# One of a block's seven products becomes seven quarter-size products, with partial sums copied inside PSUM

## The chip, the core and the metric

The kernel runs on one core of a Trainium2 chip. Its time is the device time of one execution in microseconds (us); the median of several runs counts. A core has TensorE (PE, matrix products into PSUM), VectorE (DVE), ScalarE (ACT), GpSimd (POOL) and SyncE (SP, which here issues most DMA transfers). Each engine works through its own queue in order; semaphores make one wait for another.

## The reference

The input x is 32 images of 14x14 points with 512 channels, all float32. Only the first half of the computation matters for the change; it ends in a residual sum, a group norm and a grouped 3x3 convolution.

```python
for i in range(18):                                   # on the group-normed x
    nx = gelu(einsum('bhwc,cd->bhwd', x, block_w[i]) + block_b[i])   # 512 x 512
    if i in (11, 14, 17):                             # targets
        pooled = nx.mean(axis=(1, 2))
        h = gelu(pooled @ fc1_w[t] + fc1_b[t])
        gates = softmax((h @ fc2_w[t] + fc2_b[t]).reshape(-1, 3, 512), axis=1)
        nx = nx + gammas[t] * einsum('bac,bahwc->bhwc', gates, anchors)
    x = nx
    if i in (1, 4, 9):                                # anchors
        anchors.append(x)
```

## The kernel before

**Tiling.** Channels lie on the partitions, in four chunks of 128. A tile is two images, N = 392 points; a pair is two tiles, and there are 8 pairs. A "quarter" is an SBUF tile of 128 partitions x 2 chunks x 392 points: `q[h][n]` is half h of the channels of tile n. A pair's activations are thus a 2x2 array of quarters, and a 512x512 weight is a 2x2 array of 256x256 corners `a11, a12, a21, a22`. `qpool` holds 38 quarters, `ps_b` 6 banks of PSUM.

**A block** is one layer i for one pair p: a 2x2 by 2x2 product, done in seven products instead of eight (Strassen's scheme in Winograd's form). `sums(k, j)` makes the four weight sums `s[0..3]` on VectorE for pair 0 and stores them; later pairs load them from `skeep`. `pre_adds` makes the four activation sums `t[0..3]` of the next block on VectorE, each from two quarters or from a quarter and an earlier sum. `block(k)` then issues the seven products; each is 4 matmuls of 128x128 by 128x392 (2 output chunks d x 2 input chunks kk), and each float32 matmul shows in the trace as two instructions. The sums of products are kept in PSUM banks X, Y, Z or copied to SBUF by ScalarE (`save`, line 473) and added there by VectorE (`add`, line 477); `gelu` (lines 453 and 460) writes the new quarters. In a target block `gelu` works by image, so that it can sum up the pooled values.

**Order.** `steps` lists all 144 blocks, pairs interleaved, and one step without a block (GAP). A block has 7 ticks, and after each product `run(tick)` issues whatever a calendar holds for that tick: loading and norming of the next pair, the gates of the target blocks (`gate_hidden`, `gate_logits`, `gate_softmax`, `gate_base`, `gate_part`, `gate_last`, `gate_add`), statistics and stores of a finished pair, building of the convolution's weights, and the convolution's units (`unit_load`, `unit_taps` with tile `cps`, `unit_sum`, `unit_out`). `put` finds the first tick with room for a task:

```python
ROOM = {"dve": (1.7, 0.0, 3.4, 3.4, 1.7, 0.0, 0.0), "act": (1.0, 0.8, 1.5, 1.5, 1.0, 0.8, 0.8)}
```

These are microseconds of VectorE and ScalarE for each of the 7 ticks. Inside a tick the order in which the program issues is the order in each queue.

**Head and drain.** The first pair is loaded, turned by TensorE (tile `tpi`), its statistics are taken, and the scale is a power on POOL followed by one Newton step on VectorE; 20 small matmuls (`warm`) are issued before the first block. After the last block `drain()` orders the remaining gates, norm and convolution units with a list scheduler. For chunks named in `BYPE` the output is turned by TensorE (`turn_out`, tile `tpo`) and stored in whole rows by `store_rows`; for the others VectorE transposes it (`unit_out`) and eight or so smaller stores follow.

Of the kernel before, what the change touches and what calls it, by code (L numbers as in the profile page):

```python
# [8 lines left out]

F32 = mybir.dt.float32  # L10
AF = mybir.ActivationFunctionType
ALU = mybir.AluOpType
# [7 lines left out]
def kernel(  # L20
# [20 lines left out]
    nc = tc.nc  # L41
    P = 128
    B, H, W, C = x.shape
    HW = H * W
# [27 lines left out]
    qpool = ctx.enter_context(tc.tile_pool(name="qpool", bufs=38))  # L72
    tmp = ctx.enter_context(tc.tile_pool(name="tmp", bufs=6))
    inpool = ctx.enter_context(tc.tile_pool(name="inpool", bufs=3))
# [40 lines left out]

    ROOM = {"dve": (1.7, 0.0, 3.4, 3.4, 1.7, 0.0, 0.0), "act": (1.0, 0.8, 1.5, 1.5, 1.0, 0.8, 0.8)}
    TAIL = {"dve": 3.0, "act": 3.6}
# [114 lines left out]

    def scales_newton(d, lo=0, hi=NR):
        ve, y, e, mr = d["ve"][:, lo:hi], d["y"][:, lo:hi], d["e"][:, lo:hi], d["mr"]
        nc.vector.tensor_mul(e, y, y)
        nc.vector.tensor_mul(e, e, ve)
        nc.vector.tensor_scalar(e, e, -0.5, 1.5, ALU.mult, ALU.add)
        nc.vector.tensor_mul(mr[:, 1, lo:hi], y, e)
        nc.vector.scalar_tensor_tensor(
            mr[:, 2, lo:hi], mr[:, 0, lo:hi], -1.0, mr[:, 1, lo:hi], ALU.mult, ALU.mult  # L240
        )
# [104 lines left out]
    def plan_start(p):  # L346

        t0 = NP7 * at_step[p, 0]
        parts = [(2 * p + n, c) for n in range(2) for c in range(NCK)]
        NIN = 3  # L350
        a = t0 - LEAD
        at(a - 30, copy_in, p)
        turned = []
        b = 0
        for j, (t, c) in enumerate(parts):
            at(t0 - LEAD - 6 if j < NIN else turned[j - NIN], load_blocks, t, c)
            turned.append(put(max(a, turned[j - NIN] + 4 if j >= NIN else 0), {"dve": 0.45 + c % NH * 0.15}, turn_blocks, t, c))
            a = turned[j]
        for j, (t, c) in enumerate(parts):
            b = max(b, put(turned[j // NH * NH + NH - 1], {"dve": 0.7}, stats_in, t, c))  # L360
        b = put(b + 1, {"dve": 0.8}, lambda: whole(scales_mean(pst[p])))
        b = put(b + 1, {"dve": 0.2}, lambda: whole(scales_rstd(pst[p])))
        b = put(b + 2, {"dve": 0.8}, lambda: scales_newton(pst[p]))
        e = b
        for c in range(NCK):
            e = max(e, put(b, {"dve": 1.6}, norm_in, p, c))
        b = e

        assert b < t0
        at(t0 - 1, take_start, p)  # L370

# [33 lines left out]

    def pre_adds(p, name):

        q = cur[p]
        t = ts[p] = []
        for j in range(4):  # L410
            t.append(quarter(f"t{j}_{name}"))
            i0, i1 = [
                lambda: (q[0][1], q[0][0]),
                lambda: (q[1][1], t[0]),
                lambda: (q[1][1], q[0][1]),
                lambda: (q[1][0], t[1]),
            ][j]()
            nc.vector.tensor_tensor(t[j], i0, i1, ALU.subtract)  # L418

    def block(k):  # L420
        p, i = steps[k]
        if i == GAP:
            for tick in range(NP7 * k, NP7 * (k + 1)):
                run(tick)
            pre_adds(steps[k + 1][0], f"{k + 1}")
            return
        name = f"{p}_{i}"
        tick = NP7 * k
        w = wts.pop(k)
        s, q, t = w["s"], cur[p], ts[p]  # L430
        dst = [[None, None], [None, None]]
# [4 lines left out]

        def product(acc, lhsT, rhs, first):
            for d in range(NH):
                for kk in range(NH):
                    nc.tensor.matmul(  # L440
                        acc[d][:, :N], lhsT=lhsT[:, kk, d * P : (d + 1) * P],
                        rhs=rhs[:, kk, :], start=first and kk == 0, stop=kk == NH - 1,
                        skip_group_check=not first,
                    )

# [24 lines left out]

        def save(cs, acc):
            for d in range(NH):
                nc.scalar.copy(cs[d], acc[d][:, :N])  # L473

        def add(cs, acc):
            for d in range(NH):
                nc.vector.tensor_tensor(cs[d], acc[d][:, :N], cs[d], ALU.add)  # L477

        X = bank("x")
        product(X, w["a11"], q[0][0], True)  # L480
        c1 = temps(1)
        save(c1, X)
        run(tick)
        Y = bank("y")
        product(Y, w["a12"], q[1][0], True)
        add(c1, Y)
        gelu(0, 0, c1)
        run(tick + 1)
        product(X, s[1], t[1], False)
        c2 = temps(2)  # L490
        save(c2, X)
        run(tick + 2)
        Z = bank("z")
        product(Z, s[0], t[0], True)
        c3 = temps(3)
        save(c3, Z)
        run(tick + 3)
        product(X, s[2], t[2], False)
        add(c3, X)
        gelu(1, 1, c3)  # L500
        run(tick + 4)
        product(Z, s[3], q[1][1], False)
        add(c2, Z)
        gelu(0, 1, c2)
        run(tick + 5)
        product(X, w["a22"], t[3], False)
        gelu(1, 0, [X[d][:, :N] for d in range(NH)])
        cur[p] = dst
        run(tick + 6)
        if k + 1 < len(steps) and steps[k + 1][1] != GAP:  # L510
            pre_adds(steps[k + 1][0], f"{k + 1}")
        if i in ANCHORS:
# [161 lines left out]
    def plan_head(p, i):  # L674
# [19 lines left out]
        a = t1 + 2  # L694
        while room("dve", a) < 2.2:
            a += 1
        at(a, gate_logits, k, name, box)
        return put(a, {"dve": 2.2}, lambda: whole(gate_softmax(ti, name, box)))

# [223 lines left out]
    def unit_taps(m, u):  # L923
# [3 lines left out]
        for g in range(2):  # L927
            xv = d["xs"][:, g, 1].rearrange("p (b h) -> p b h", h=H)
            pv = ps[:, g * 2 * NV : (g + 1) * 2 * NV].rearrange("p (b h) -> p b h", h=H)
            for j, dy in enumerate((1, 0, 2)):  # L930
                lo, hi = max(0, 1 - dy), min(H, H + 1 - dy)
                nc.tensor.matmul(  # L932
                    pv[:, :, lo:hi], lhsT=bw[:, g, dy],
                    rhs=xv[:, :, lo + dy - 1 : hi + dy - 1],
                    start=j == 0, stop=j == 2, skip_group_check=True,
                )
# [51 lines left out]

    def store_rows(m, c):
        nc.scalar.dma_start(  # L990
            out[m * BI : (m + 1) * BI, :, :, c * P : (c + 1) * P].rearrange("b h w d -> (b h) w d"),
            outs.pop((m, c)),
        )
# [15 lines left out]
    done = []  # L1009

    def plan_unit(m, u, tk, ahead, stay=False):
        b = tk - ahead
# [5 lines left out]
        a = max(b + 2, tk)  # L1018
        while room("dve", a + 1) < 0.65:
            a += 1  # L1020
        at(a, unit_taps, m, u)
        b = put(a + 1, {"dve": 0.65}, unit_sum, m, u)
        b = put(b, {"dve": 0.6}, unit_out, m, u)
        done.append((a, b))
# [34 lines left out]
    def drain():  # L1059
# [47 lines left out]
        for c in range(NCK):  # L1107
# [40 lines left out]
            else:  # L1148
                for p, d in ((PK, dk), (PL, dl)):
# [11 lines left out]
                  nbytes=0.8e6)  # L1161
        xs, outp, ofirst, BYPE = [], [], None, (2, 3, 4)
        for mm, u in [(m - 1, u) for u in range(NGAP, NU)] + [(m, u) for u in range(NU)]:
# [29 lines left out]
            if ul == UC - 1 and (mm - (NBAT - 2)) * NCK + c not in BYPE:  # L1193
# [8 lines left out]
                if ofirst:  # L1202
                    ofirst.free = t
            elif ul == UC - 1:
                ofirst.free = Task(
                    "ACT", 0.6, lambda mm=mm, c=c: store_rows(mm, c), [o], nbytes=0.8e6
                )
# [56 lines left out]


    for s in range(TS):
        for n in range(2):
            load_in(n, s, qpool, "q", nc.sync if n == 0 else nc.scalar)
    load_block(0)
    brow = load_biases()  # L1270
    for b in range(NI):
# [3 lines left out]
        for n in range(2):  # L1275
            for c in range(NCK):
                stats_in(n, c, (b,))
    whole(scales_mean(pst[0]))
    whole(scales_rstd(pst[0]))
    for j in range(4):  # L1280
        sums(0, j)
    turn_biases(brow)

    warm = aux("warm")
    for j in range(20):
        nc.tensor.matmul(warm[:, :P], lhsT=ident, rhs=gmask, start=True, stop=True)  # L1286
    scales_newton(pst[0])
    for c in range(NCK):
        norm_in(0, c, (0,), nc.vector)
        norm_in(0, c, (1,), nc.scalar)  # L1290
    take_start(0)
    pre_adds(0, "0")


    NGAP = 6
    LEAD = 42
    for k in range(len(steps)):
# [5 lines left out]
        if k > 0:  # L1303
            at(NP7 * (k - 1), load_block, k)
            for tk, j in ((4, 0), (4, 1), (4, 2), (5, 3)) if p == 0 else ((2, 1), (3, 0), (4, 2), (5, 3)):
                at(NP7 * (k - 1) + tk, sums, k, j)
            if p == 0:
                left["dve"][NP7 * (k - 1) + 4] = 0.0
        if i in TARGETS:
            at(NP7 * (k - 1 if k == len(steps) - 1 else k) + 4, load_gates, k)  # L1310
            for tk, us in enumerate((0.8, 0.0, 1.5, 1.5, 0.5, 0.0, 0.0)):
                left["act"][NP7 * k + tk] = us
# [4 lines left out]
    for p in range(NPAIR):  # L1317
        plan_differences(p)
        for i in TARGETS[:-1]:
            a = plan_gates(p, i, plan_head(p, i), [[0, 1], [2, 3]])  # L1320
            assert a < NP7 * at_step[p, i + 1], (p, i, a, NP7 * at_step[p, i + 1])
    for p in range(NPAIR):
# [53 lines left out]
```

## Time and profile before

| | us |
|---|---|
| median of 3 runs | 2941.75 (2938.26 to 2943.97) |
| the profiled execution's own time | 2944.35 |
| its span | 2942.6 |
| TensorE busy in the span | 2905.9 |
| VectorE busy | 1827.2 |
| ScalarE busy | 1425.1 |
| first product starts at | 22.57 |
| last product ends at | about 2836.7 |

The page of a profile gives busy times of the engines, the chain of work that ended last, and groups of like instructions with their source line. The list of waits says which engine's instruction waited for what: microseconds in all, times, longest. The timeline lists instructions in order, runs of like ones merged: start, duration, engine, line, operation, output<-inputs, shape, count, and in brackets the idle time before it with what ended it. Matmuls overlap, so that the distance between two starts says more than the duration. PEld is TensorE's loading of weights; it runs beside PE.

### The profile page before, as it was taken

Reading aid. Unit: us, or ns where it says so; the run is one execution under the profiler, and the core shown is the slowest. Engines: PE = TensorE matmul, PEld = TensorE weight load, DVE = VectorE, ACT = ScalarE, POOL = GpSimd, SP = SyncE. Lnnn points to the kernel's source line nnn. Section 1 sums busy time; section 2 is a strip of 40 time slices with the busy share of each in tenths; the row PEclk is TensorE's granted clock in tenths of the full one; section 3 lists DMA queues with packets and bytes.
Section 4 is the critical chain, followed back from the end, with each engine's and each line's share of the span. In section 5 each row is a group of like instructions: output and inputs, shape, how many; then the busy total and the mean of one; then the engine's idle time right before and its main releaser. Section 6 shows DMA issues by size and latency. Waiting matters only on the chain.

```text
span 2942.6 us, 31539 instructions
## 1 busy us (share of the span) xinstructions
PE 2905.9 (99%) x9693; PEld 1775.3 (60%) x9693; DVE 1827.2 (62%) x3512; ACT 1425.1 (48%) x3281; POOL 78.4 (3%) x60
## 2 busy tenths in 40 slices
PE   9999999999999999999999999999999999999997
PEld 5555555555555665666666666666665655556666
DVE  6887777755377454774547745576455763545676
ACT  4445455555455454454544544445455454544551
POOL 0000000000000000000000000000000000000000
PEclk9999999999999999999999999999999999999999
DMA  5544455644565455654657546566465753443676
GB/s 183 164 148 152 163 171 151 189 124 127 154 168 180 128 173 163 184 162 131 185 151 187 169 138 183 142 190 169 130 189 149 182 150 115 126 148 107 189 211 159
DMA packets 471817, 469.44 MB, mean 160 GB/s; under 512 B 237555, under 2 KB 300130, under 8 KB 471650
## 3 DMA queue, kind: packets, MB, share of 16 engines
q1 hardware_dynamic: 458482, 449.77, 51.5%
q0 software_dynamic: 4608, 12.85, 2.5%
q10 hardware_dynamic: 8560, 4.82, 0.6%
q8 instruction: 78, 1.28, 0.2%
q14 instruction: 89, 0.73, 0.1%
HBM read 388.29 MB, written 90.28 MB: 163 GB/s over the span
## 4 chain that ended last, share of the span: by engine, by line
PE 97%; DMA 2%; DVE 1%; issue 0%; ACT 0%; SPq 0%; DVEq 0%
PE x L440 51%; PE z L440 26%; PE y L440 13%; PE cps L932 4%; PE lps L571 1%; DMA x<-x2d 1%; PE hps L554 1%; DMA w<-in_L_conv_fc_w_dram 0%; PE warm L1286 0%; PE tpi L309 0%; DVE x L921 0%; PE mps_b L208 0%; PE tpo L972 0%; PE mps_a L208 0%; PE vps_a L208 0%
## 5 line engine op out<-in xcount | busy, mean ns | idle before, releaser
L440 PE MATMUL x<-t,s 128*128 128x392 f32 x2304 | 809.8, 494 | 0.0
L453 ACT ACTIVATE o<-c,bias 128x392 f32<-128x392 f32 x720 | 437.3, 620 | 656.1 <-DVE c L477 648.5
L440 PEld LDWEIGHTS x<-t,s 128*128 128x128 f32 x2304 | 433.5, 190 | 302.2 <-issue 0.5
L477 DVE TENSOR_TENSOR c<-x,c 128x392 f32<-128x392 f32 x288 | 160.4, 565 | 486.2 <-PE x L440 411.3
L473 ACT COPY c<-x 128x392 f32<-128x392 f32 x576 | 278.2, 484 | 352.1 <-PE x L440 347.4
L440 PE MATMUL x<-t,w 128*128 128x392 f32 x1152 | 403.2, 493 | 0.0
L440 PE MATMUL z<-t,s 128*128 128x392 f32 x1152 | 402.9, 492 | 0.0
L440 PE MATMUL z<-o,s 128*128 128x392 f32 x1088 | 380.9, 493 | 0.0
L440 PE MATMUL y<-o,w 128*128 128x392 f32 x1088 | 380.4, 492 | 0.0
L440 PE MATMUL x<-o,w 128*128 128x392 f32 x1088 | 380.3, 492 | 0.0
L440 PEld LDWEIGHTS z<-t,s 128*128 128x128 f32 x1152 | 218.6, 190 | 158.8 <-DMA s<-skeep 0.7
L440 PEld LDWEIGHTS x<-t,w 128*128 128x128 f32 x1152 | 218.4, 190 | 158.6
L477 DVE TENSOR_TENSOR c<-y,c 128x392 f32<-128x392 f32 x288 | 162.1, 565 | 237.1 <-PE y L440 147.5
L418 DVE TENSOR_TENSOR t<-o,o 128x784 f32<-128x784 f32 x272 | 264.1, 971 | 65.8 <-ACT o L453 63.9
L440 PEld LDWEIGHTS y<-o,w 128*128 128x128 f32 x1088 | 206.6, 190 | 151.1
L440 PEld LDWEIGHTS x<-o,w 128*128 128x128 f32 x1088 | 206.6, 190 | 148.9
L440 PEld LDWEIGHTS z<-o,s 128*128 128x128 f32 x1088 | 206.2, 190 | 149.5
L418 DVE TENSOR_TENSOR t<-o,t 128x784 f32<-128x784 f32 x272 | 264.4, 972 | 4.7
L473 ACT COPY c<-z 128x392 f32<-128x392 f32 x288 | 139.6, 485 | 203.9 <-PE z L440 203.8
L477 DVE TENSOR_TENSOR c<-z,c 128x392 f32<-128x392 f32 x288 | 156.4, 560 | 95.0 <-PE z L440 94.7
L460 ACT ACTIVATE o<-c,bias 128x196 f32<-128x196 f32 x288 | 129.5, 450 | 92.9 <-DVE c L477 92.4
L453 ACT ACTIVATE o<-x,bias 128x392 f32<-128x392 f32 x240 | 136.7, 581 | 68.2 <-PE x L440 62.8
(119 smaller groups left out, 2027.0 us busy)
## 6 DMA issues: line engine op xcount, KB each, us to landing
w<-in_L_conv_block_w_dram SPq DMA_DIRECT2D x144, 1024.0 KB
s<-skeep SPq DMA_DIRECT2D x504, 256.0 KB
x2d<-xc SPq DMA_DIRECT2D x116, 224.0 KB
x<-x2d SPq DMA_DIRECT2D x104, 224.0 KB
skeep<-s SPq DMA_DIRECT2D x72, 256.0 KB
xkeep<-xt SPq DMA_DIRECT2D x32, 392.0 KB
o<-xkeep POOLq DMA_DIRECT2D x32, 392.0 KB, 6.0
bw<-band SPq DMA_DIRECT2D x32, 384.0 KB
```

What stands on the lines that cost most here:

```text
L418: nc.vector.tensor_tensor(t[j], i0, i1, ALU.subtract)
L440: nc.tensor.matmul(acc[d][:, :N], lhsT=lhsT[:, kk, d * P : (d + 1) * P], rhs=rhs[:, kk, :], start=first and kk == 0, stop=kk == NH - 1, sk ...
L453: nc.scalar.activation(o[:, d, :], srcs[d], AF.Gelu_apprx_tanh, bias=bias[:, r : r + 1])
L460: nc.scalar.activation(o[:, d, sl], srcs[d][:, sl], AF.Gelu_apprx_tanh, bias=bias[:, r : r + 1], accum_out=pooled[:, c, m : m + 1],)
L473: nc.scalar.copy(cs[d], acc[d][:, :N])
L477: nc.vector.tensor_tensor(cs[d], acc[d][:, :N], cs[d], ALU.add)
L554: nc.tensor.matmul(hps[:, :NB4], lhsT=w1[:, kk, :], rhs=box["pooled"][:, kk, :], start=(kk == 0), stop=(kk == NCK - 1),)
L571: nc.tensor.matmul(lps[:, m * NB4 : (m + 1) * NB4], lhsT=w2[:, m * P : (m + 1) * P], rhs=h, start=True, stop=True,)
L932: nc.tensor.matmul(pv[:, :, lo:hi], lhsT=bw[:, g, dy], rhs=xv[:, :, lo + dy - 1 : hi + dy - 1], start=j == 0, stop=j == 2, skip_group_chec ...
```

## The change

Product s0 x t0 is itself a 2x2 by 2x2 product: `s[0]` is cut into four 128x128 corners `a`, `t[0]` into four corners `b` of 128x196 (a half h of the points, chunk kk). It is done by the same scheme in seven inner products of 128x128 by 128x196. For that four weight sums `u` (`inner_sums`, kept in `ukeep` for later pairs) and four activation sums `v` (in `pre_adds`) are needed. Partial sums stay in PSUM: ScalarE copies X to Y and one corner of Z to another, and TensorE adds the next products onto the copies. The second product is added onto Y, so that `gelu(0, 0)` reads PSUM and the temporaries c1 and their VectorE adds are gone. One partial sum, f, goes to SBUF and is added to both corners of Z's second bank by VectorE.

With it: t0 and v of the next block are made before the seventh product instead of after it; `tmp` has 4 buffers for 6; the calendar's `ROOM` and due times are other; convolution units go only into ticks 1 to 4 of a block, and their bank is cleared once; the first pair's scale comes from an integer guess and three Newton steps on VectorE; six warm-up matmuls of 392 columns replace 20 of 128; the last chunk's output is turned by TensorE and stored in two halves.

```diff
-    tmp = ctx.enter_context(tc.tile_pool(name="tmp", bufs=6))
+    tmp = ctx.enter_context(tc.tile_pool(name="tmp", bufs=4))
...
-    ROOM = {"dve": (1.7, 0.0, 3.4, 3.4, 1.7, 0.0, 0.0), "act": (1.0, 0.8, 1.5, 1.5, 1.0, 0.8, 0.8)}
+    ROOM = {"dve": (3.3, 1.9, 1.4, 1.8, 1.4, 0.6, 0.0), "act": (1.5, 0.75, 0.75, 0.8, 1.5, 1.5, 1.5)}
...
+    def scales_guess(d):
+        ps = group_sums(f"vps_{d['name']}", d["dv"], NR)
+        yield
+        nc.vector.tensor_scalar(d["ve"], ps, 1.0 / HW, 1e-5, ALU.mult, ALU.add)
+        nc.vector.tensor_scalar(
+            d["y"].bitcast(I32), d["ve"].bitcast(I32), -0.5, float(0x5F3759DF), ALU.mult, ALU.add
+        )
+    def scales_newton(d, lo=0, hi=NR, times=1):
         ve, y, e, mr = d["ve"][:, lo:hi], d["y"][:, lo:hi], d["e"][:, lo:hi], d["mr"]
-        nc.vector.tensor_mul(e, y, y)
-        nc.vector.tensor_mul(e, e, ve)
-        nc.vector.tensor_scalar(e, e, -0.5, 1.5, ALU.mult, ALU.add)
-        nc.vector.tensor_mul(mr[:, 1, lo:hi], y, e)
+        for i in range(times):
+            nc.vector.tensor_mul(e, y, y)
+            nc.vector.scalar_tensor_tensor(e, e, -0.5, ve, ALU.mult, ALU.mult)
+            o = y if i < times - 1 else mr[:, 1, lo:hi]
+            nc.vector.scalar_tensor_tensor(o, e, 1.5, y, ALU.add, ALU.mult)
...
-        assert b < t0
-        at(t0 - 1, take_start, p)
+        assert b < t0 - 1
+        at(t0 - 2, take_start, p)
...
+    ukeep = [tc.dram_tile([P, 4 * P], F32, name=f"ukeep{i}") for i in range(NB)]
+    def inner_sums(k):
+        p, i = steps[k]
+        d = wts[k]
+        u = d["u"] = spool.tile([P, 4, P], F32, tag="u", name=f"u_{k}")
+        if p > 0:
+            nc.sync.dma_start(u.rearrange("p j d -> p (j d)"), ukeep[i])
+            return
+        a = corners(d["s"][0], P)
+        for j, (i0, i1) in enumerate((
+            (a[1][0], a[0][0]), (a[1][1], u[:, 0]), (a[1][1], a[1][0]), (a[0][1], u[:, 1]),
+        )):
+            nc.vector.tensor_tensor(u[:, j], i0, i1, ALU.subtract)
+        nc.sync.dma_start(ukeep[i], u.rearrange("p j d -> p (j d)"))
+    def corners(t, n):
+        return [[t[:, kk, h * n : (h + 1) * n] for kk in range(NH)] for h in range(2)]
+    def pre_adds(p, q, name, js):
+        t = ts.setdefault(p, {})
+        for j in js:
+            t[j] = quarter(f"t{j}_{name}")
             i0, i1 = [
                 lambda: (q[0][1], q[0][0]),
                 lambda: (q[1][1], t[0]),
...
                 lambda: (q[1][0], t[1]),
             ][j]()
             nc.vector.tensor_tensor(t[j], i0, i1, ALU.subtract)
+            if j == 0:
+                v = t["v"] = quarter(f"v_{name}").rearrange("p k (n x) -> p (k n) x", x=HW)
+                b = corners(t[0], HW)
+                for l, (i0, i1, op) in enumerate((
+                    (b[1][0], b[1][1], ALU.add), (v[:, 0], b[0][0], ALU.subtract),
+                    (b[0][0], b[1][0], ALU.subtract), (b[0][1], v[:, 1], ALU.subtract),
+                )):
+                    nc.vector.tensor_tensor(v[:, l], i0, i1, op)
...
+        def part(acc, d, lhsT, rhs, first=False):
+            for kk in range(NH):
+                nc.tensor.matmul(
+                    acc[d][:, :N], lhsT=lhsT[:, kk, d * P : (d + 1) * P],
+                    rhs=rhs[:, kk, :], start=first and kk == 0, stop=kk == NH - 1,
+                    skip_group_check=True,
+                )
+        def product(acc, lhsT, rhs):
             for d in range(NH):
-                for kk in range(NH):
-                    nc.tensor.matmul(
-                        acc[d][:, :N], lhsT=lhsT[:, kk, d * P : (d + 1) * P],
-                        rhs=rhs[:, kk, :], start=first and kk == 0, stop=kk == NH - 1,
-                        skip_group_check=not first,
-                    )
+                part(acc, d, lhsT, rhs)
...
-        def save(cs, acc):
-            for d in range(NH):
-                nc.scalar.copy(cs[d], acc[d][:, :N])
+        def save(cs, acc, ds=range(NH)):
+            for d in ds:
+                nc.scalar.copy(cs[d][:, :N], acc[d][:, :N])
         def add(cs, acc):
             for d in range(NH):
                 nc.vector.tensor_tensor(cs[d], acc[d][:, :N], cs[d], ALU.add)
+        a, b, u, v = corners(s[0], P), corners(t[0], HW), w["u"], t["v"]
+        Z = []
+        def corner(d, n):
+            return Z[d][:, n * HW : (n + 1) * HW]
+        def inner(d, n, lhsT, rhs, first=False):
+            nc.tensor.matmul(
+                corner(d, n), lhsT=lhsT, rhs=rhs, start=first, stop=True, skip_group_check=True
+            )
         X = bank("x")
-        product(X, w["a11"], q[0][0], True)
-        c1 = temps(1)
-        save(c1, X)
+        Y = bank("y")
+        for d in range(NH):
+            part(X, d, w["a11"], q[0][0], True)
+            save(Y, X, (d,))
+        Z += bank("z")
+        inner(1, 0, u[:, 0], v[:, 0], True)
+        inner(1, 1, a[0][0], b[0][0])
+        f = tmp.tile([P, N], F32, tag="c", name=f"f_{name}")[:, :HW]
+        nc.scalar.copy(f, corner(1, 0))
+        nc.scalar.copy(corner(0, 0), corner(1, 1))
         run(tick)
-        Y = bank("y")
-        product(Y, w["a12"], q[1][0], True)
-        add(c1, Y)
-        gelu(0, 0, c1)
+        part(Y, 0, w["a12"], q[1][0])
+        inner(0, 0, a[0][1], b[0][1])
+        inner(1, 1, u[:, 1], v[:, 1])
+        nc.scalar.copy(corner(1, 0), corner(1, 1))
+        part(Y, 1, w["a12"], q[1][0])
+        gelu(0, 0, [Y[d][:, :N] for d in range(NH)])
         run(tick + 1)
-        product(X, s[1], t[1], False)
         c2 = temps(2)
-        save(c2, X)
+        part(X, 0, s[1], t[1])
+        save(c2, X, (0,))
+        inner(1, 0, a[1][1], v[:, 3])
+        inner(1, 1, u[:, 2], v[:, 2])
+        nc.scalar.copy(corner(0, 1), corner(1, 1))
         run(tick + 2)
-        Z = bank("z")
-        product(Z, s[0], t[0], True)
+        part(X, 1, s[1], t[1])
+        save(c2, X, (1,))
+        inner(0, 1, u[:, 3], b[1][1])
+        both = Z[1][:, :N].rearrange("p (n x) -> p n x", n=2)
+        nc.vector.tensor_tensor(
+            both, both, f.unsqueeze(1).to_broadcast([P, 2, HW]), ALU.add
+        )
         c3 = temps(3)
         save(c3, Z)
         run(tick + 3)
-        product(X, s[2], t[2], False)
+        product(X, s[2], t[2])
         add(c3, X)
         gelu(1, 1, c3)
         run(tick + 4)
-        product(Z, s[3], q[1][1], False)
+        product(Z, s[3], q[1][1])
         add(c2, Z)
         gelu(0, 1, c2)
         run(tick + 5)
-        product(X, w["a22"], t[3], False)
+        pn = steps[k + 1][0] if k + 1 < len(steps) and steps[k + 1][1] != GAP else None
+        if pn is not None:
+            qn = dst if pn == p else cur[pn]
+            pre_adds(pn, qn, f"{k + 1}", (0,))
+        product(X, w["a22"], t[3])
         gelu(1, 0, [X[d][:, :N] for d in range(NH)])
         cur[p] = dst
         run(tick + 6)
-        if k + 1 < len(steps) and steps[k + 1][1] != GAP:
-            pre_adds(steps[k + 1][0], f"{k + 1}")
+        if pn is not None:
+            pre_adds(pn, qn, f"{k + 1}", (1, 2, 3))
...
-                    start=j == 0, stop=j == 2, skip_group_check=True,
+                    start=g == 0 and j == 0, stop=j == 2, skip_group_check=True,
...
+    def fits(tick):
+        return steps[tick // NP7][1] == GAP or 1 <= tick % NP7 <= 4
...
+        while not fits(a) or room("dve", a + 1) < 0.65:
...
-        xs, outp, ofirst, BYPE = [], [], None, (2, 3, 4)
+        xs, outp, ofirst, BYPE = [], [], None, (2, 3, 4, 7)
...
+            elif u == NU - 3 and mm == m:
+                Task("ACT", 0.6, lambda mm=mm, c=c: store_rows(mm, c, 0, P // 2), [o], nbytes=0.4e6)
...
+    def keep_busy(n):
+        for j in range(n):
+            banks.append(ps_b.tile([P, 512], F32, tag="b", name="warm"))
+            nc.tensor.matmul(
+                banks[-1][:, :N].rearrange("p (j x) -> p j x", j=NCK), lhsT=ident,
+                rhs=ident[:, : N // NCK].unsqueeze(1).to_broadcast([P, NCK, N // NCK]),
+                start=True, stop=True,
+            )
+    keep_busy(3)
...
-    whole(scales_mean(pst[0]))
-    whole(scales_rstd(pst[0]))
-    for j in range(4):
+    for j, parts in enumerate((scales_mean(pst[0]), scales_guess(pst[0]))):
+        next(parts)
         sums(0, j)
+        whole(parts)
+    scales_newton(pst[0], times=3)
     turn_biases(brow)
-
-    warm = aux("warm")
-    for j in range(20):
-        nc.tensor.matmul(warm[:, :P], lhsT=ident, rhs=gmask, start=True, stop=True)
-    scales_newton(pst[0])
-    for c in range(NCK):
-        norm_in(0, c, (0,), nc.vector)
-        norm_in(0, c, (1,), nc.scalar)
+    keep_busy(3)
+    for n in range(2):
+        for c in range(NCK):
+            norm_in(0, c, (n,), nc.vector if (c + n) % 2 == 0 else nc.scalar)
     take_start(0)
-    pre_adds(0, "0")
+    pre_adds(0, cur[0], "0", range(4))
+    inner_sums(0)
+    for j in range(2, 4):
+        sums(0, j)
...
-    LEAD = 42
+    LEAD = 47
...
-            for tk, j in ((4, 0), (4, 1), (4, 2), (5, 3)) if p == 0 else ((2, 1), (3, 0), (4, 2), (5, 3)):
+            for tk, j in ((3, 0), (3, 1), (4, 2), (5, 3)):
                 at(NP7 * (k - 1) + tk, sums, k, j)
+            at(NP7 * (k - 1) + 4, inner_sums, k)
             if p == 0:
-                left["dve"][NP7 * (k - 1) + 4] = 0.0
+                for tk, us in ((3, 0.5), (4, 0.0), (5, 0.0)):
+                    left["dve"][NP7 * (k - 1) + tk] = us
...
-            for tk, us in enumerate((0.8, 0.0, 1.5, 1.5, 0.5, 0.0, 0.0)):
+            for tk, us in enumerate((1.2, 0.0, 0.3, 0.8, 0.3, 0.2, 0.0)):
```

## The prediction

> **What bounds the kernel now.** I read the page first, then TensorE's waits, then stretches of the timeline. The page:
>
> ```profile
> span 2942.6 us, 31539 instructions
> ...
> PE 2905.9 (99%) x9693; PEld 1775.3 (60%) x9693; DVE 1827.2 (62%) x3512; ACT 1425.1 (48%) x3281; POOL 78.4 (3%) x60
> ...
> PE 97%; DMA 2%; DVE 1%; issue 0%; ACT 0%; SPq 0%; DVEq 0%
> ```
>
> TensorE is busy for 99% and the chain that ended last is 97% TensorE; VectorE and ScalarE have 38% and 52% to spare. A busy TensorE could still hide stalls, so its waits:
>
> ```profile
> PE cps L932 <- DMA x<-x2d: 10.8, 4, 6.2
> PE tpi L309 <- DMA xin<-in_x_dram: 4.2, 1, 4.2
> PE cps L932 <- DVE x L921: 3.0, 4, 1.2
> ```
>
> The list has no product of a block (L440): the largest waits lie in the head (tpi) and the drain (cps), before 22.6 us and after 2836 us. In the 144 blocks the time is TensorE's own streaming. What a pass costs is read from the distance between starts, since the durations overlap:
>
> ```profile
> 998.74 2.33 PE L932 MATMUL cps<-x,bw 128*128 128x224 f32 x12
> 1000.91 2.80 PE L440 MATMUL x<-t,s 128*128 128x392 f32 x8
> ...
> 1008.81 2.80 PE L440 MATMUL x<-o,w 128*128 128x392 f32 x8
> ...
> 1010.38 0.49 ACT L473 COPY c<-x 128x392 f32<-128x392 f32 x1 [0.78 <-PE x L440]
> ...
> 1011.44 2.80 PE L440 MATMUL y<-o,w 128*128 128x392 f32 x8
> ...
> 1298.42 1.84 PE L571 MATMUL lps<-h,w 128*128 128x4 f32 x16
> ...
> 1300.13 2.88 PE L440 MATMUL x<-t,s 128*128 128x392 f32 x8
> ```
>
> A product is 8 instructions (4 float32 matmuls, two passes each): 1011.44-1008.81 = 2.63 us, 329 ns a pass of 392 columns. A conv unit is 12 passes, 4 of 224 and 8 of 208 columns, mean 213.3: 2.17 us, 181 ns. The lps passes, 4 columns, follow each other in 1.71/16 = 107 ns: that is the floor that a weight load sets. So above the floor a pass costs its columns: (329-181)/(392-213.3) = 0.83 ns a column, about 4 ns fixed.
>
> **The change, part by part.**
>
> *Streaming.* Gone in each block: product s0 x t0, 8 passes of 392 columns, 2.63 us. New: 7 matmuls of 196 columns, 14 passes. By the line above 196 columns cost 181-17.3x0.83 = 166 ns, over the 107 floor; 14x166 = 2.33 us. Saved 0.30 to 0.31 us (rounding of the starts), over 144 blocks 43 to 45; I take 44 us.
>
> Here a rule speaks against the change. The Trainium skill, "TensorE: Matmul & The Clock Gate", section "What overlaps and what doesn't", has a weight load overlap running matmuls only if they use other row groups; all of these use the full array. Then every pass pays load and stream, with the page's load of 128/1.2 = 107 ns: 14x(107+163) = 3.78 against 8x(107+327) = 3.47 us, a loss of 0.31 us a block, 45 us in all. The rows decide: a load is listed for every pass, yet 392 columns take 329 ns, not 434, and the conv passes 181, not 285, though six more short passes a block are just where it would hurt. I use the rows.
>
> *New waits on ScalarE.* Before, no product waited closely for ScalarE. Now a12 x q10 is added onto ScalarE's copy Y, and an inner product onto a copied quarter of Z. Count from the block's start T: a11 ends T+2.63; two inner products T+3.29; Y's first half T+4.61; two more inner T+5.27; Y's second half T+6.59. A copy starts 0.26 us after its last pass has left the issue (1010.38, against 1008.81+4x0.329 = 1010.13). A copy of 392 columns takes 0.48; one of 196 has as nearest row L314's 0.34, 0.31 in sequence. PSUM as the target has no row; I bound it by 0.2 and 0.6 and take 0.31. So Y's halves are there at T+2.1 and T+3.4, f at T+3.9, the corner copy at T+4.2. The first is wanted at T+3.29, the corner at T+4.61: slack 0.4 us, the thinnest in every block. The later corner copies wait behind `gelu` and calendar work and still have over 0.7 us. So nothing stalls in an ordinary block. Behind these waits TensorE's own queue stands, and with it everything.
>
> *Gate blocks.* ScalarE's room in ticks 4, 5 and 6 goes from 1.0, 0.8 and 0.8 to 1.5: two `gate_last` in each instead of one. The block after a target, before:
>
> ```profile
> 1302.74 0.25 DVE L607 SCALAR_TENSOR_TENSOR g<-ex,gam,ssum 128x32 f32<-128x32 f32 x1
> ...
> 1303.70 1.03 DVE L477 TENSOR_TENSOR c<-x,c 128x392 f32<-128x392 f32 x2
> ...
> 1304.30 1.13 ACT L453 ACTIVATE o<-c,bias 128x392 f32<-128x392 f32 x2 [2.18 <-DVE c L477]
> ...
> 1305.34 0.79 ACT L656 ACTIVATE gq<-o,g 128x196 f32<-128x196 f32 x2
> ...
> 1307.28 0.79 ACT L656 ACTIVATE gq<-o,g 128x196 f32<-128x196 f32 x2
> ...
> 1307.98 1.04 ACT L453 ACTIVATE o<-x,bias 128x392 f32<-128x392 f32 x2
> ...
> 1308.92 0.80 ACT L656 ACTIVATE gq<-o,g 128x196 f32<-128x196 f32 x2
> ...
> 1309.68 0.49 ACT L473 COPY c<-x 128x392 f32<-128x392 f32 x1
> ```
>
> ScalarE runs nearly gap-free from the first gelu on, and its copy at 1309.68 comes just when its half product is ready (1308.11, the block's start, +1.32+0.26). With a double `gate_last` (1.50 us in the trace) three times: add at 1303.0 (no gate_part before it now), gelu 1303.6-1304.75, gates to 1306.2, gelu to 1307.35, gates to 1308.8, gelu to 1309.8, gates to 1311.25, save Y to 1311.75. The next block starts at 1308.11, so Y's half is wanted at 1311.4: a stall of 0.4 us with the handing over. There are 23 such blocks (16 for targets 11 and 14, 7 for 17): +9 us; ends 0 (gates an instruction earlier) and 25 (softmax or an add 0.6 us later).
>
> *VectorE.* Gone: two adds onto c1 (0.565 each). New: four v of 196 columns, one add over both corners (0.56, like L477), for pair 0 also four u of 128. From L418 (784: 971 ns) and L664 (392: 561) a 196-column add is 0.36, some 0.28 back to back. Net +0.6 us a block of 18.1, for pair 0 +1.4. VectorE is busy 59% in 800-1200 us and 79% in 31-260 (pair 0): it becomes about 62% and 89%. t0 and v move ahead of the seventh product: gelu(0,1) ends 1.1 us before the next block, t0 takes 0.9, v 1.1, so v is there at T+0.9 and wanted at T+2.63. With its room filled (0.6 us in tick 5) T+1.5. For pair 0 the four u and two sums stand in front of the adds; the same count gives T+1.4. Priced at 0, covered by 1.1 us of slack; ends 0 and +8.
>
> *Queues.* SP issues one more load a block (u, 256 KB, 0.32 us like L395), 33 MB in all on 469; pair 0 stores u instead. It stands behind s2, waiting for the third last product, so 7 us ahead of its use; s3 and the next w behind it move 0.3 us. The load of s0 moves to tick 3, a block ahead. Moved calendar work (fits, LEAD 47) changes no TensorE sum. A conv unit in tick 1 may wait for Y's bank, 0.1 us for some 8 of 32. POOL loses one power at the start. All 0, ends 0 and +5.
>
> *Head.* The first product starts at 22.57 us, after 40 warm-up passes (15.85-22.57). POOL's 3.29 us power is replaced by nine VectorE steps of 0.2, so the scales come near 18.0 instead of 20.2. But inner product one needs t0, all four t's, v and u0 in VectorE's order: q01 at 20.8, then 0.9+1.0+2.7+0.2 gives 25.6, and TensorE waits for it. That equals a start at 23.0: +0.5 (ends -2, +2; the first `keep_busy` can delay tpi by 1.3).
>
> *Tail.* Outputs of the last four units go over TensorE and ScalarE: from the last sum 0.7+0.8+0.6 us to the store, in place of 1.15 of transposes and four issues of 0.85-1.0; but the rows of 256 B are as many as 512 B rows, and such a store took 4 to 5 us. -0.5 (ends -3, +2).
>
> Sum: -44+9+0+0+0.5-0.5 = -35. The profiled execution was 2944.35 (span 2942.6 and 1.75 around it), 2.6 above the median; the difference taken from the median: 2907.
>
> **The rivals.**
> *No stall anywhere*: the gates come earlier, -44: 2898. For it: today's list of waits is empty in the blocks. Against: the gap-free ScalarE row above.
> *More cover lost* (VectorE late with v in pair 0, a slot of the 38 quarters late because v takes one more, ScalarE full in more blocks): 2915 to 2935.
> *A stall in every block, slower than before.* Mechanism: f and the corner copy, on ScalarE between the inner products. From 1.32 us of cover 0.31 goes to handing over; the copies may take 1.01 together. Past 0.30 us more, 0.66 each, the saving is gone. At 0.9 each the stall is 0.79 us, net +0.49x144 = +70, 3012. Against: a 392-column copy takes 0.48, so half of it should not take 0.66; only the write into PSUM is unseen.
> *It doesn't do what it says*: the same skill's "PSUM — Partial Sum Buffer" (The four PSUM rules) says that ScalarE's writes set no written-bit, so a matmul after such a seed adds only where an earlier matmul left the bit. Six warm-up banks and the conv's single start fit that; no row here shows it, and the time would be the same.
>
> **How the numbers follow.** Gate stalls only, 0.45 (2907, own range 2902 to 2914); no stall 0.25 (2898, with the head's and tail's good ends 2893); more cover lost 0.16; a stall in every block 0.10; within 0.2% (2936 to 2948, what this measurement can tell) 0.04. Faster 0.86, same 0.04, slower 0.10. The range 2893 to 2932 takes in the first three but for the extremes.
>
> **What would show it.** Right: inner passes 166 ns apart; blocks of 18.1 us where 18.43 was; TensorE waits under 15 us in all on ScalarE, each before Y after a gate block. Wrong: passes over 188 ns apart (14x188 = 2.63); a wait on corner copies in every block; products waiting for v, or for u's load.

## The result: slower by 0.6%, and the profile after

The changed kernel took 2958.5 us (median of 4 runs, 2957.2 to 2960.9) against 2942.9 before; the ratio is 1.0056, with a 95% interval of 1.0044 to 1.0069. Forecast was 2907, range 2893 to 2932. Span for span it is 2959.1 against 2942.6 us, 16.5 more.

The page of the changed kernel, span, busy times and the chain that ended last by engine and by line:

```profile
span 2959.1 us, 33809 instructions
...
PE 2881.7 (97%) x10545; PEld 1898.2 (64%) x10545; DVE 1933.8 (65%) x3996; ACT 1548.2 (52%) x3865; POOL 78.7 (3%) x59
...
PE 91%; DMA 5%; SPq 2%; DVE 2%; issue 1%; ACT 0%; POOL 0%; DVEq 0%; POOLq 0%; ACTq 0%
PE x L482 48%; PE y L482 13%; PE z L482 12%; PE z L533 11%; PE cps L1013 4%; DMA u<-ukeep 2%; DMA x<-x2d 1%; PE lps L652 1%; SPq L275 1%; PE hps L635 1%; SPq L282 0%; DMA w<-in_L_conv_fc_w_dram 0%; DMA s<-skeep 0%; DVE t L452 0%; DMA bq<-band 0%
```

TensorE is busy for 24 us less in a span 16.5 us longer, so it idles some 40 us more. And the chain names lines that it did not name before: `u<-ukeep`, the load of the weight sums of the inner product, and SP's queue at L275 and L282, which are `load_blocks`, the small loads of the next pair. TensorE's largest waits (us in all, times, longest):

```profile
PE z L533 <- DMA u<-ukeep: 36.7, 11, 6.3
PE cps L1013 <- DMA x<-x2d: 10.4, 3, 7.4
PE z L533 <- DVE u L433: 3.2, 1, 3.2
```

L533 is the inner product. It waited for u's load in 11 of the 126 blocks that load it, up to 6.3 us. (`cps` lies in the drain and had such a wait before too; the third line is the first block's u.) An ordinary block of the changed kernel, from its timeline:

```profile
1006.17 2.80 PE L482 MATMUL x<-o,w 128*128 128x392 f32 x8
...
1007.74 0.47 ACT L519 COPY y<-x 128x392 f32<-128x392 f32 x1 [0.78 <-PE x L482]
...
1008.80 0.49 PE L533 MATMUL z<-v,u 128*128 128x196 f32 x2
...
1009.13 0.49 PE L533 MATMUL z<-t,s 128*128 128x196 f32 x2
...
1009.47 1.48 PE L482 MATMUL y<-o,w 128*128 128x392 f32 x4
1009.72 0.32 ACT L548 COPY f<-z 128x196 f32<-128x196 f32 x1 [0.19 <-PE z L533]
1009.94 0.33 ACT L549 COPY z<-z 128x196 f32<-128x196 f32 x1
```

An inner matmul (two passes) starts 0.33 us after the last: 166 ns a pass, as forecast. The copy of X to Y takes 0.47 us, a corner of 196 columns copied inside PSUM 0.33; the corner copy ends at 1010.27 and is wanted at 1010.78. There is no stall. Now a block that waits. First SP's queue ahead of it, then TensorE:

```profile
1132.74 1.97 SPq L406 DMA_DIRECT2D s<-skeep  x2
1134.76 2.04 SPq L275 DMA_DIRECT2D xb<-xcol  x4
1138.20 3.31 SPq L282 DMA_DIRECT2D xr<-xcol  x4
1141.56 4.01 SPq L275 DMA_DIRECT2D xb<-xcol  x8
1145.61 2.24 SPq L282 DMA_DIRECT2D xr<-xcol  x4
1147.95 0.37 SPq L406 DMA_DIRECT2D s<-skeep  x1
1148.37 0.43 SPq L427 DMA_DIRECT2D u<-ukeep  x1
```

```profile
1151.55 0.99 PE L533 MATMUL z<-v,u 128*128 128x196 f32 x2 [6.32 <-DMA u<-ukeep]
1152.33 0.86 PE L533 MATMUL z<-t,s 128*128 128x196 f32 x2
1152.99 2.82 PE L482 MATMUL y<-o,w 128*128 128x392 f32 x4
1155.60 0.86 PE L533 MATMUL z<-t,s 128*128 128x196 f32 x2
```

Between s0, s1 (L406, tick 3) and s2, u (tick 4) stand 20 small loads, some 0.5 us apiece and with waits of their own in between. The block starts at 1142.4; u is issued at 1148.4, 14 us after s1, and is there 3.2 us later; TensorE had wanted it at about 1145.2. And the wait costs more than itself: the four passes from 1152.99 take 2.61 us, 653 ns each in place of 329. The stretches of this block (PE, PEld, DVE, ACT and POOL in order; then the clock granted to TensorE, the busy share of the DMA engines, GB/s):

```profile
1125.50:1143.60 18.10, 18.10 (x63) 11.44 (x62) 7.73 (x14) 8.60 (x18) 0.00 (x0) 1.00 0.83 186
1143.60:1151.50 7.90, 1.62 (x5) 0.58 (x4) 3.81 (x6) 0.94 (x2) 0.00 (x0) 0.73 0.56 129
1151.50:1157.00 5.50, 5.45 (x13) 4.22 (x14) 0.00 (x0) 0.55 (x2) 0.00 (x0) 0.50 0.94 276
```

The block before takes 18.10 us at full clock, as forecast. After 6 us of idling, TensorE is granted half its clock for the next 5.5 us.

### The profile page after: what moved, and what is told of

It reads as the page before. It is cut to its first block, busy times and chain, and to the rows that moved or that the text cites. A ratio compares the mean times of both kernels' runs of the same rounds, so it can differ in the third digit from the quotient of the medians.

```text
span 2959.1 us, 33809 instructions
## 1 busy us (share of the span) xinstructions
PE 2881.7 (97%) x10545; PEld 1898.2 (64%) x10545; DVE 1933.8 (65%) x3996; ACT 1548.2 (52%) x3865; POOL 78.7 (3%) x59
## 4 chain that ended last, share of the span: by engine, by line
PE 91%; DMA 5%; SPq 2%; DVE 2%; issue 1%; ACT 0%; POOL 0%; DVEq 0%; POOLq 0%; ACTq 0%
PE x L482 48%; PE y L482 13%; PE z L482 12%; PE z L533 11%; PE cps L1013 4%; DMA u<-ukeep 2%; DMA x<-x2d 1%; PE lps L652 1%; SPq L275 1%; PE hps L635 1%; SPq L282 0%; DMA w<-in_L_conv_fc_w_dram 0%; DMA s<-skeep 0%; DVE t L452 0%; DMA bq<-band 0%
## 5 line engine op out<-in xcount | busy, mean ns | idle before, releaser
L482 PE MATMUL x<-t,s 128*128 128x392 f32 x2304 | 833.3, 494 | 0.3 <-ACT c L519 0.3
L499 ACT ACTIVATE o<-c,bias 128x392 f32<-128x392 f32 x480 | 291.8, 620 | 353.4 <-DVE c L523 353.3
L482 PE MATMUL y<-o,w 128*128 128x392 f32 x1088 | 410.8, 501 | 0.0
L569 DVE TENSOR_TENSOR z<-z,f 128x392 f32<-128x392 f32 x144 | 82.6, 574 | 363.1 <-ACT z L563 363.0
L519 ACT COPY c<-x 128x392 f32<-128x392 f32 x288 | 139.8, 485 | 300.0 <-PE x L482 300.0
L533 PE MATMUL z<-v,u 128*128 128x196 f32 x864 | 218.7, 335 | 44.0 <-DMA u<-ukeep 36.7
L519 ACT COPY y<-x 128x392 f32<-128x392 f32 x288 | 133.7, 469 | 175.9 <-PE x L482 174.6
L533 PEld LDWEIGHTS z<-v,u 128*128 128x128 f32 x864 | 158.2, 193 | 89.0 <-issue 52.5
L499 ACT ACTIVATE o<-y,bias 128x392 f32<-128x392 f32 x240 | 141.3, 590 | 53.3 <-PE y L482 53.3
```

Source lines behind the costliest of these rows:

```text
L482: nc.tensor.matmul(acc[d][:, :N], lhsT=lhsT[:, kk, d * P : (d + 1) * P], rhs=rhs[:, kk, :], start=first and kk == 0, stop=kk == NH - 1, sk ...
L499: nc.scalar.activation(o[:, d, :], srcs[d], AF.Gelu_apprx_tanh, bias=bias[:, r : r + 1])
L519: nc.scalar.copy(cs[d][:, :N], acc[d][:, :N])
L533: nc.tensor.matmul(corner(d, n), lhsT=lhsT, rhs=rhs, start=first, stop=True, skip_group_check=True)
L569: nc.vector.tensor_tensor(both, both, f.unsqueeze(1).to_broadcast([P, 2, HW]), ALU.add)
```

## The experiments

My theory after this: the shorter passes give their 44 us, and u's load comes too late because SP's queue, which works in order, is held by other transfers ahead of it. Rivals: the DMA engines are too full, wherever a load is queued; or it is not u but VectorE's v that is late.

**u one tick earlier.** One line of the planning loop:

```diff
-            at(NP7 * (k - 1) + 4, inner_sums, k)
+            at(NP7 * (k - 1) + (4 if p == 0 else 3), inner_sums, k)
```

> u's load of pairs 1 to 7 is issued in tick 3, right behind s0 and s1, instead of tick 4; nothing else changes. Theory (SP's queue is too late with u: in the six worst blocks 4 to 12 issues of xb and xr of 0.47 us, or other loads, stand between s1 and u): the waits of inner products for u fall from 47 us to some 10, those left being the blocks where s1 itself is issued late (81 and 117 by number), the half-speed passes behind the long waits go too, and the time falls to about 2912 (2903 to 2922). Rival 1 (the DMA engines are too full, so the 256 KB come late whenever they are asked for): the loads land only a little earlier, the waits stay over 30 us, time 2940 to 2955. Rival 2 (the waits come from VectorE's v, not from u): no change, 2959.

Measured: 2921.1 us (2913 to 2931), ratio to before 0.9928 (0.9903 to 0.9952). u's wait in the list of its profile:

```profile
PE z L533 <- DMA u<-ukeep: 12.2, 5, 3.0
```

Down from 36.7 us by passing nothing but SP's own transfers of ticks 3 and 4. The two rivals said 2940 and more. In four of the five waits left u is issued 0.5 to 1.5 us after its block's start; in the fifth it is issued 2.8 us before it and takes 7.6 us to be there, against 3.2 in the block above.

**u on POOL's queue,** in tick 4 as in the changed kernel:

```diff
-            nc.sync.dma_start(u.rearrange("p j d -> p (j d)"), ukeep[i])
+            nc.gpsimd.dma_start(u.rearrange("p j d -> p (j d)"), ukeep[i])
```

> u's load stays in tick 4 but is issued by POOL's queue, which has almost nothing else to do. Theory (SP's queue): POOL waits only for u's buffer, so the load starts right after the last inner product of the block before; no wait for u in any block, time 2895 to 2905, which would be the full 44 us of shorter passes less some 2 us of head and tail. Rival 1 (DMA engines full): the same bytes go through the same engines at nearly the same time, so the waits stay over 30 us, 2940 to 2955. Rival 2 (v): 2959.

Measured: 2911.6 us (2907.4 to 2913.1), ratio 0.9891 (0.9877 to 0.9906): the largest single step, 47 us, though 7 us above the range that I expected. The same bytes go from the same place to the same place, in the same tick of the program; only the queue differs. In its list of waits u's load is gone; of the inner products' waits for operands the head's u from VectorE (3.9 us, once) and s0 are left:

```profile
PE z L533 <- DMA s<-skeep: 1.9, 2, 1.4
```

So full DMA engines are not the whole cause. As a part of it they are not ruled out, since the edit does two things. On POOL's queue u does not stand behind s2 either, and is issued 7.4 us before its block's start in the median, where SP issues it 4.7 us before; and none of its landings is slow enough to be waited for:

```profile
DMA to landing us min/median/max: 3.0/3.7/7.3
```

The Trainium skill bears on this ("DMA: Bandwidth & Descriptors", section "Issuing engines are not separate DMA queues"): another engine's queue brings no bandwidth, only the sequencer's time of issuing, usually small beside the transfer. By that the edit should be worth 0.43 us a load at most and nothing where it is hidden. No run here measures the bandwidth of one queue. But what the edit saves is not this load's issue: it is all that the in-order queue issues and waits for ahead of it, 14 us in the block above.

**The bursts off SP, u left where it was:** both `dma_start` of `load_blocks`

```diff
-            nc.sync.dma_start(
+            nc.gpsimd.dma_start(
...
-                nc.sync.dma_start(xr[q * TB : (q + 1) * TB], cols[q, N - TB :, c : c + NH])
+                nc.gpsimd.dma_start(xr[q * TB : (q + 1) * TB], cols[q, N - TB :, c : c + NH])
```

> u untouched; the small loads of the next pair (xb, xr) are issued by POOL's queue instead of SP's. Theory (SP's queue held by these bursts): the six blocks in which the burst stands just ahead of u lose their wait (about 29 us of 47, plus the half-speed passes behind), the ones with convolution or x2d transfers ahead keep part; time about 2915 (2905 to 2930), unless POOL's slower issue makes the next pair itself late. Rival 1 (DMA engines full): no gain, 2950 to 2965.

Measured: 2929.1 us, with a wide spread that I did not explain (2915 to 2936; the profiled execution took 2921), ratio 0.9943 (0.9922 to 0.9963). u's waits are down by two thirds:

```profile
PE z L533 <- DMA u<-ukeep: 13.1, 9, 2.4
```

So the bursts are what made SP issue u late: in this trace u is never issued later than 1.6 us before its block's start. The waits that are left are of a second kind. Those over 0.3 us belong to loads that were issued 2.5 to 4.7 us before the block and were there only 7.4 to 10 us after their issue, with the DMA engines' busy share at 1.0.

**u one tick later,** tick 5, behind s3.

> u's load of pairs 1 to 7 is issued one tick later, in tick 5 behind s3. Theory (issue time of u decides): u is issued 2.6 us later in each of 126 blocks; from the margin seen (an undisturbed load is issued 7 us ahead and takes some 3 us to land) ordinary blocks still just hold, and every block with transfers ahead waits 2.6 us longer or begins to wait: 80 to 200 us more, 3020 to 3150. Rival 2 (v): no change, 2959.

Measured: 3012.0 us (3001 to 3022), ratio 1.0234 (1.0206 to 1.0262), somewhat below the range that I expected:

```profile
PE z L533 <- DMA u<-ukeep: 80.0, 22, 9.3
```

With ticks 3, 4 and 5 the waits for u in the list go 12.2, 36.7, 80.0 us and the time 2921, 2959, 3012: they follow the moment of issue. The rival v is out as well; it was never moved.

**Another LEAD.** LEAD says how many ticks ahead the next pair is loaded: 42 before, 47 in the change. 42 does not fit the new plan, so I tried 50.

```diff
-    LEAD = 47
+    LEAD = 50
```

> The changed kernel with LEAD 50 instead of 47: the next pair's loads start three ticks earlier, so its bursts of xb and xr fall on other ticks; u stays on SP in tick 4. Theory (whatever stands ahead of u in SP's queue): bursts still meet u in some blocks, only in others; waits for u stay between 20 and 70 us, time 2930 to 2980. If it was only LEAD 47 that set the bursts just ahead of u by accident, the waits nearly go and the time falls below 2915.

Measured: 2940.3 us (2931 to 2946), ratio 0.9998 (0.9989 to 1.0007), so 18 us faster than the change with nothing else touched:

```profile
PE z L533 <- DMA u<-ukeep: 24.2, 9, 4.3
```

In this trace no u is issued later than 0.8 us before its block's start: the bursts no longer hold its issue, so that where they fall is worth 18 us. What is left is the second kind: the nine loads were issued 0.8 to 2.8 us before the block and were there 6.0 to 8.6 us after their issue.

**The kernel before with one more load.** 256 KB a block that nobody reads, in tick 4 behind s2 (and `tmp` with 4 buffers, to make room):

```diff
+    def extra_load(k):
+        u = spool.tile([P, 4, P], F32, tag="u", name=f"u_{k}")
+        nc.sync.dma_start(
+            u.rearrange("p j d -> p (j d)"), skeep[steps[k][1]][0][:, : 4 * P]
+        )
...
+            if p > 0:
+                at(NP7 * (k - 1) + 4, extra_load, k)
```

> The kernel before with one more load of 256 KB a block (126 in all) that nobody reads, issued by SP in tick 4 behind s2, with tmp cut to 4 buffers to make room for it. Theory (a load hurts only through who waits for it): no product waits, time 2938 to 2948, as before. Rival 1 (bytes and DMA engines): loads that the blocks do read come late, waits of products for DMA over 10 us, time over 2955.

Measured: 2945.8 us, ratio 1.0014 (1.0003 to 1.0024), some 3 us. Its list of TensorE's waits names no product of a block. So 33 MB more on the same queue cost next to nothing by themselves; they cost when a product reads them soon. In its trace the extra load too is issued late: in 8 of the 126 blocks after the block's start, by 1.2 to 9.4 us. Had a product wanted it 2.6 us into the block, it would have waited.

**s0 on POOL too, and the head in another order.** On top of u on POOL's queue:

```diff
+            (nc.gpsimd if j == 0 else nc.sync).dma_start(s[j].rearrange("p k d -> p (k d)"), skeep[i][j])
...
-    pre_adds(0, cur[0], "0", range(4))
+    pre_adds(0, cur[0], "0", (0,))
     inner_sums(0)
+    pre_adds(0, cur[0], "0", (1, 2, 3))
```

> The POOL-queue kernel with two more edits: s0 of pairs 1 to 7, which the inner products now need five microseconds earlier than before, is also loaded by POOL's queue, and in the head the four u of the first block are made right behind t0 and v, ahead of t1, t2 and t3. Theory: the first inner product no longer waits some 4 us in the head (2.7 us gained, and the clock stays up), and the waits for s0 (1.9 us) go: 2911.6 less about 5, that is 2903 to 2908. If s0's place in SP's queue is not what makes it late, the s0 waits stay and only the head's part is seen, 2907 to 2910.

Measured: 2903.2 us (2898.4 to 2904.4), ratio 0.9868 (0.9852 to 0.9885). Both waits are gone or small. The head of the changed kernel, and below it the first inner product of this one:

```profile
24.88 0.97 DVE L452 TENSOR_TENSOR t<-xt,t 128x784 f32<-128x784 f32 x1
25.76 0.29 DVE L433 TENSOR_TENSOR u<-s 128x128 f32<-128x128 f32 x1
...
26.20 0.57 PE L533 MATMUL z<-v,u 128*128 128x196 f32 x2 [3.23 <-DVE u L433]
```

```profile
23.57 0.57 PE L533 MATMUL z<-v,u 128*128 128x196 f32 x2 [0.56 <-DVE u L433]
```

VectorE made three t that nobody needed yet before the u that TensorE stood waiting for: 2.6 us.

**u made by VectorE in every pair,** with no load and no store of u, and the head in the new order:

```diff
-        if p > 0:
-            nc.sync.dma_start(u.rearrange("p j d -> p (j d)"), ukeep[i])
-            return
...
-        nc.sync.dma_start(ukeep[i], u.rearrange("p j d -> p (j d)"))
...
-            at(NP7 * (k - 1) + 4, inner_sums, k)
+            at(NP7 * (k - 1) + (4 if p == 0 else 6), inner_sums, k)
```

> No load of u at all: VectorE makes the four u in every pair, from s0, in tick 6 behind t0 and v (0.8 us a block more for VectorE, 33 MB less read); the head's order as in the other kernel of this call. Theory: with the late transfer gone the full gain of the shorter passes shows, if VectorE's four adds are done by the time the first inner product starts (v at T+0.9, u at T+1.7, wanted at T+2.6): 2900 to 2912. If VectorE is the next bound, inner products wait for u on VectorE instead, over 10 us in the list: 2915 to 2945.

Measured: 2900.5 us (2897.8 to 2903.4), ratio 0.9865 (0.9850 to 0.9879), the fastest of all. From its page, and the one wait for u that its list has (another, of 2.2 us for v, comes once, behind the step without a block):

```profile
PE 2865.8 (99%) x10545; PEld 1887.6 (65%) x10545; DVE 2041.7 (70%) x4500; ACT 1548.4 (53%) x3865; POOL 78.7 (3%) x59
```

```profile
PE z L528 <- DVE u L429: 1.0, 3, 0.5
```

TensorE is back at 99%, and VectorE, now at 70%, is in time with u but for 1.0 us in all. With no load of u the change is 42 us faster than the kernel before; the head's other order is part of that.

## Why the prediction was wrong

The forecast summed to -35 us; the spans differ by +16.5. By its steps:

*Streaming, -44: right.* Passes of 196 columns are 166 ns apart, an undisturbed block takes 18.10 to 18.12 us for 18.43, and with u made by VectorE the stretch from block 1 to the last block is 2754.6 us where it was 2795.6, 41 less. The rule of "What overlaps and what doesn't", which the prediction sets against the change, would also have made it slower, but passes 166 ns apart are not what it gives: it was not the reason.

*Queues, "7 us ahead of its use", priced 0 with ends 0 and +5: this is the step that failed.* It cost about 59 us. From block 1's first product to the end of the last block, before and after (the stretch's length, then TensorE's busy time):

```profile
40.84:2836.39 2795.55, 2793.01 (x9130) 1677.68 (x9129) 1736.61 (x3276) 1384.05 (x3173) 68.91 (x46) 1.00 0.55 159
41.76:2852.15 2810.39, 2766.74 (x9987) 1802.19 (x9986) 1845.17 (x3759) 1504.13 (x3745) 72.49 (x46) 0.99 0.59 171
```

The stretch grew by 14.8 us, where 143 blocks should have shrunk it by 44. TensorE's idle time in it went from 2.5 to 43.7 us: 41 us are waits. Its busy time fell by 26 us instead of 44: 18 us are slower passes, most of them at half clock behind those waits. Of the waiting, 39.6 us stand before the first inner product of 12 blocks: the list's 36.7, and one wait of 2.9 us that it puts down to VectorE's o, which that product does not read.

The count of 7 us was right for an ordinary block: in the median u is issued 4.7 us before its block and wanted 2.6 us into it. It failed in those 12, in two ways. In six, u was issued 2.2 to 5.9 us after the block's start, behind the bursts; these waits sum to 27.8 us. In the other six it was issued at least 1.7 us before the block, but was there only 4.8 to 8.1 us after its issue; these sum to 11.7 us. One of the second kind, SP's issue, the product, and the stretch between them:

```profile
1590.92 0.42 SPq L427 DMA_DIRECT2D u<-ukeep  x1
1598.97 0.57 PE L533 MATMUL z<-v,u 128*128 128x196 f32 x2 [2.92 <-DMA u<-ukeep]
1590.92:1598.97 8.05, 5.13 (x17) 2.70 (x15) 7.42 (x18) 2.74 (x5) 0.61 (x1) 1.00 1.05 325
```

The DMA engines are busy throughout (share 1.05, 325 GB/s). So the rival of full engines holds for the smaller part. Whether POOL's queue also shortens the landing, no run here tells apart from the earlier start that it brings.

I had counted u's issue from an SP queue with nothing in it but the blocks' own loads, though that queue also carries the calendar's bursts, each behind waits of its own. The lateness was there before, hidden, and the trace before shows it. In 8 of 126 blocks s2, in whose tick u was put, is issued after its block's start; the latest by 7.6 us (block start, then s2):

```profile
1223.42 2.80 PE L440 MATMUL x<-o,w 128*128 128x392 f32 x8
1230.99 1.65 SPq L395 DMA_DIRECT2D s<-skeep  x1
```

But s1 was wanted 5.3 us into its block, s0 7.9 and s2 10.5; u is wanted after 2.6. (The load that moved for pairs 1 to 7 is s1, from tick 2 to 3; s0 was in tick 3 already.) "Moved calendar work changes no TensorE sum" fell with it: three ticks of LEAD are worth 18 us.

*Gate blocks, +9: no stall, mis-sized by about 0.5 us.* ScalarE in the block after a target, in the changed kernel:

```profile
835.30 1.49 ACT L737 ACTIVATE gq<-o,g 128x196 f32<-128x196 f32 x4
836.69 1.04 ACT L499 ACTIVATE o<-x,bias 128x392 f32<-128x392 f32 x2
837.63 1.50 ACT L737 ACTIVATE gq<-o,g 128x196 f32<-128x196 f32 x4
839.03 0.86 ACT L519 COPY y<-x 128x392 f32<-128x392 f32 x2
...
839.74 1.48 PE L482 MATMUL y<-o,w 128*128 128x392 f32 x4
```

The order is the forecast one, with two `gate_last` in a row each time. But the chain reached its last gates about half a microsecond sooner than I had laid it out, and Y's first half, at 839.03+0.47, is there 0.2 us before TensorE wants it.

*ScalarE's copies, no stall in an ordinary block: right,* with 0.5 us of slack where I had 0.4. The rival of a stall in every block through slow copies is out (0.33 us measured, 0.66 needed).

*VectorE, 0: right,* even with u made there (70% busy). *Head, +0.5:* 0.9 at block 1, by the mechanism named. *Tail, -0.5:* +0.7 (106.2 us from the last block's end before, 106.9 after).

Of the rivals, "more cover lost" had the right shape: a transfer hidden before, no longer hidden. It named v, slots and ScalarE as the culprit, none of which was; only the last of the signs of being wrong named u's load. "No stall anywhere" (2898) is about what the kernel without that load reached (2900.5). On the rival of the seeds in PSUM no trace here speaks.

## What to carry to other kernels

When a change makes a transfer needed earlier in its stage, its slack has to be counted from when its queue can reach it: list what the same queue issues ahead of it in the worst stage, with the waits of those, not in the average one. Allow also for a slow landing: the same 256 KB were there 3.2 us after their issue in one block and 8.1 in another. The list of waits shows only today's readers; a late transfer with a patient reader does not appear. A few small loads that something is waiting for belong on a queue of their own, or are better computed by an engine with time to spare.

## What was not expected of the hardware

A wait of TensorE can cost more than its length: after 6.3 us of idling it was granted a clock of 0.50 for the next 5.5 us, with passes of 653 ns instead of 329, about 3 us more for that one wait. Of the 12 waits in the changed kernel seven have such a stretch behind them, 29.7 us in all: the five of 3.5 us and more, and two of 2.9. Another two, of 2.9 and 3.1 us, have none. The mean granted clock is 0.989 in the changed kernel and 0.996 in the fastest one.

Copies of a PSUM bank into another PSUM bank cost ScalarE 0.47 us for 392 columns, where the copy to SBUF took 0.48; a corner of 196 columns took 0.31 to 0.33.
